# Third chunk's scores by seven half products, projected rows in two copies a buffer, two or three softening steps a block

## The chip, the cores and the metric

The kernel runs on one core of one Trainium2 chip. The metric is the device time of one execution in microseconds; the median of several runs is compared. Engines are called as in the profile: PE (matmul), PEld (its weight loads), DVE (vector), ACT (scalar), POOL (GpSimd), SP or SyncE (which issues most DMAs). Everything is float32 unless said otherwise.

## The reference

A graph network of four layers over N = 2708 nodes with D = 512 features; `adj` is a sparse 0/1 matrix (about 16 neighbours a node). `_layernorm` is over the features.

```python
deg = max((adj != 0).sum(-1), 1)
x = _layernorm(x + relu((dinv * (adj + I) * dinv @ x + x) @ W0 + b0))  # layer 0, dinv = rsqrt(deg)
x = _layernorm(x + (dis * adj * dis @ x) @ W1.T + b1)                  # layer 1
y = x                                                                  # layer 2: two attention layers
for l in range(2):
    Wh, Ws = split(y @ W_stack[l], 2)
    a = softmax(Wh @ Ws.T) * adj                 # softmax over all 2708, then masked
    y = leaky_relu(a @ Wh + y, 0.01)
x = _layernorm(x + y)
x = _layernorm(x + adj @ (x @ W3) + b3)                                # layer 3, heads side by side
```

## The kernel before, in words

**Tiles.** The 2708 nodes are 22 blocks of 128 rows (the last has 20). They are also cut into six chunks of columns, `CH`: four of 512, one of 384, one of 276; indices k = 0 to 5, so the "third chunk" is k = 2. SBUF is handed out in 87 pages of 128 x 512 floats (`page`), eleven wider ones (`wide`) for gathered rows; PSUM is two groups of four banks (`bank`). `Ordered` keeps the order in which instructions are issued on each engine, so every engine runs them in the order of the Python program.

**Layers 0, 1 and 3** are products with the adjacency, chunk by chunk (`step`, `multiply`), in two float32r halves (xh and xl times m, the mask turned to float32r by ACT). `finish` and `normalizing` do the layer norm of a chunk's blocks.

**An attention layer** (`Attention.layer`) goes over the chunks of destination nodes. For a chunk, `walk` yields the score matrix, transposed, source block by source block: 22 pages `s`, 128 sources x up to 512 destinations each. A block "directly" is four matmuls (`scores`; each shows as two records in the profile), copied from PSUM by ACT. In chunks of the list `SEVEN` (before: k = 0 and 1) two blocks at a time are made by seven half products in place of eight (`pair_steps`, Strassen's scheme: `PRODUCTS`, sums s1 to s4 of the projected weights and t1 to t4 of the moving side, made or loaded once). There PE's results x (product by product) and y pass through ACT copies, and DVE adds them: `first_block` adds y from PSUM to s, `second_block` adds v to r. Block 18 and the last, of 20 rows, are done directly also there.

**What goes on beside the scores.** `walk` yields "end" after each block and, in seven-product chunks, also "mid" between products. At "end" number n, `layer` lets the chunk before (`old`) go on: maxima of its blocks (`greatest`), at n = 2 PE's transposes `tr_top` and DVE's reduction `mx` and copy `wide` (`shift_rows`), at n = 4 the transposes `tr_mx` of `wide` into a tile `shift` (`shift_columns`); then the chunk joins `to_soften`. A step of `soften` is, on DVE, a subtraction of `shift` from block v, ACT's exponential of block v - 3, DVE's sum and multiplication with the mask of block v - 4, and the store of that block (`pairs<-s`, queue of SP). A chunk needs 26 steps. How many are issued is written out by hand:

```python
if what == "mid":
    self.soften_next(); self.weigh(); continue
...
many = 2 if len(self.to_soften) > 1 else 1 + n % 2
for _ in range(0 if ch.seven else many):
    self.soften_next()
```

**Gathers.** Row j of the DRAM buffer `pairs` holds, for source j, its projected row z (512 floats) and its masked scores towards the chunk's four blocks of destinations, z standing three times between the scores so that z and any 128 scores are one piece of memory. There are two buffers a layer, used by chunks in turn; `store_z` writes z into both. When a chunk is softened wholly, `fetch` gathers with POOL's indirect DMA, 128 listed sources at a time (12 gathers for a block of destinations), up to ten ahead; `weigh` multiplies a gathered tile's scores with its z on PE into `acc`. It only does so when a clock kept by the program (`advance`) says that the tile should have landed. `end` finishes a block of destinations on DVE: times the softmax's divisor, plus the residual `xr`, leaky ReLU; in the second layer also plus the old row block x1 (`first`), loaded by `weigh` with a block's first product, and statistics.

**Ends of the layers.** In the last chunk and behind it, a generator `fill` gives PE other work: the second attention layer's projections (`second`, `project_steps`, which read the first layer's output, transposed by `turn` 8 us of program clock after a chunk's end), or layer 3's first steps (`early`). Loads for `early` go out at n = 5, 11 and 19 of the last chunk.

**Names in the profile.** All work is recorded under line 71 (a helper), so tiles are told apart by name: `sp`, `spx`, `spy` are scores, `acc<-g` gathered products, `acc<-m,xh` and `xl` layers 0, 1, 3; `wst` and `z` projections.

Of the kernel before, what the change touches and what calls it, by code (L numbers as in the profile page):

```python
# [505 lines left out]
ALONE = 18  # L506
SEVEN = [0, 1]
PROJECTED = [0, 1]
# [44 lines left out]
class Fast:  # L553
# [18 lines left out]
    def run(self):  # L572
        kernel, nc = self.k, self.nc
        with ExitStack() as ctx:
# [37 lines left out]
            for some in (parts[:-1], parts[-1:]):  # L612
                made = []
                for i, n, ps in some:
                    made.append((i, n, self.combine(ly, k, len(made), i, n, ps)))
                for _ in self.finish(ly, k, made):
                    pass
# [27 lines left out]
    def early(self, run):  # L645

        seq = run.seq
        yield True
        self.load(*seq[0])
        self.load(*seq[1])  # L650
        yield True
        self.prepare(*seq[0])
# [47 lines left out]

    def normalizing(self, mv, rows):


        nc, small = self.nc, self.small
        m = len(rows)
        y = small.tile([P, DC], FP, tag="y", name="y")[:, :m]
        yield from self.rsqrt(y, mv[:, :m, 1], LN_EPS)
        for q, (r, o, n) in enumerate(rows):
            nc.vector.tensor_scalar(
                o[:n], r[:n], mv[:n, q, 0:1], y[:n, q : q + 1], ALU.subtract, ALU.mult  # L710
            )
# [532 lines left out]

    def finish(self, ly, k, parts):
# [7 lines left out]
        work = self.normalizing(ly.mv[k], [(x, o, n) for (_, n, x), (_, o, _) in zip(parts, out)])  # L1253
# [62 lines left out]
    def step(self, run, t):  # L1316

        ly, k, g = run.seq[t]
        self.other = (k + 1) % 2
        if run.before and run.phase == 2:  # L1320
            next(run.finish)
        self.before_products(run, t)
        if ly.number == 0 and (k, g) == (1, 0):
# [101 lines left out]
    def index(self, k):  # L1425
# [74 lines left out]
        yield "PE"  # L1500
        rank = ranks("rest", rest, up)
        yield "DVE"
# [81 lines left out]
class Chunk:  # L1584


    def __init__(self, ly, k):
# [4 lines left out]
        self.half = self.cw // 2  # L1592
        self.seven = k in SEVEN
        self.part, self.complete, self.ready, self.top = {}, [], [], None
# [24 lines left out]
class Attention:  # L1619
# [7 lines left out]
    def __init__(self, fast):  # L1627
# [10 lines left out]
            [  # L1638
                self.scratch.tile([NP, 2 * PAIR + D], FP, tag=f"p{a}{b}", name=f"pairs{a}{b}")
                for b in range(2)  # L1640
# [22 lines left out]
        self.left = None  # L1663
        self.to_soften = []


    def blank(self):

        t, n = self.page("blank"), NP - N
        self.nc.gpsimd.memset(t, 0.0)  # L1670
        for pairs in (p for ly in self.pairs for p in ly):
            self.nc.sync.dma_start(
                pairs[N:, : 2 * PAIR + D].rearrange("j (r d) -> j r d", d=D),
                t[:n, :].unsqueeze(1).to_broadcast([n, (2 * PAIR + D) // D, D]),
            )
# [176 lines left out]
    def store_z(self, ly, i, n, z):  # L1852
        for b in range(2):
            rows = ly.pairs[b][i * P : i * P + n, :]
            self.nc.sync.dma_start(
                bass.AP(rows.tensor, rows.offset, [rows.ap[0], (PAIR, 3), (1, D)]),
                z[:n].unsqueeze(1).to_broadcast([n, 3, D]),
            )
# [40 lines left out]
    def in_turn(self, pairs, a, b, ly=None, k=None):  # L1899
# [7 lines left out]
        for n, what in enumerate(order):  # L1907
# [4 lines left out]
            else:  # L1912
# [3 lines left out]
                if not t["left"]:  # L1916
                    t["left"] = "-"
                    self.total(t)
                    for i, z in zip(t["blocks"], t["to"]) if ly else ():
                        self.store_z(ly, i, P, z)  # L1920
            if n == len(order) - 4 and ly:
                self.sum_xt(ly, k + 1)
# [160 lines left out]
    def pair_steps(self, ch):  # L2083
# [6 lines left out]
        groups = [p[0] for p in pairs if p[0] < STREAMED and p[1] == 0]  # L2090
        following = ch.k + 1 in SEVEN

# [18 lines left out]
        def six(t):  # L2111
            self.product(ch, t, 3, t["y"][:, h:cw])
            self.product(ch, t, 6, t["x"])
            nc.scalar.copy(t["s"][:, h:cw], t["x"])

        def seven(t):
# [9 lines left out]
        def first_block(t):  # L2126
            nc.vector.tensor_add(t["s"][:, :cw], t["s"][:, :cw], t["y"][:, :cw])
            ch.complete.append(t["j"][0])
# [5 lines left out]
        for n, p in enumerate(pairs):  # L2134
# [9 lines left out]
            if older:  # L2144
                four(older)
            if ch.k and p[1] == 0 and p[0] + 1 in groups:
                self.load_sums(ch.ly, p[0] + 1)
            if following and p == pairs[-2]:
                self.load_sums(ch.ly, 0)
# [134 lines left out]
    def soften(self, ch):  # L2284
# [30 lines left out]
        to = ch.ly.pairs[ch.k % 2][j * P : j * P + n, :]  # L2315
        if cw == BANK:
            nc.sync.dma_start(
                to[:, : 2 * PAIR].rearrange("j (r x) -> j r x", x=PAIR)[:, :, D:],
                ch.s[j][:n, :].rearrange("j (r x) -> j r x", x=2 * P),
            )  # L2320
            return
        for r in range(2):
            w = min(2 * P, cw - r * 2 * P)
            nc.sync.dma_start(
                to[:, r * PAIR + D : r * PAIR + D + w],
                ch.s[j][:n, r * 2 * P : r * 2 * P + w],
            )

# [16 lines left out]
    def fetch(self, ch):  # L2345
# [6 lines left out]
        for b in (q, q + 1):  # L2352
            self.load_rows(ch, b)

        h = t // ONLY if t < QUARTERS * ONLY else (QUARTERS - 1, 0)[q % 2]
        first, width = (D + P + h * QW, D + P - h * QW) if q % 2 else (0, D + (h + 1) * QW)
        self.nc.gpsimd.indirect_dma_start(
# [39 lines left out]
    def weigh(self, wait=False):  # L2397
# [16 lines left out]
        if first:  # L2414
            ch.acc = self.bank(1, f"acc{ch.name}_{q}")
            if ch.ly.number == 1:
                ch.first[q] = self.page(f"x1{ch.name}_{q}")
                self.nc.sync.dma_start(ch.first[q][:w], self.k.saved[1][ch.blocks[q][0]][:w])
        for h, g in enumerate(gs):
            lo, m = (0, w) if len(gs) == 1 else (h * QW, QW)  # L2420
            e, z = (0, P - lo) if q % 2 else (D + lo, 0)
            nc.tensor.matmul(
# [13 lines left out]
    def end(self, ch, q, acc, x, first):  # L2436
# [19 lines left out]
        if q == len(ch.blocks) - 1:  # L2456
            self.later(
                8,
                lambda: self.f.turn(
                    ch.ends, ch.k, 1, f"x2b{ch.k}", self.k.turned[1][ch.k], nc.sync  # L2460
                ),
            )

# [60 lines left out]
    def layer(self, ly, chunks, fill):  # L2524
        f = self.f
        self.chunks, self.made = chunks, {}
        for k, ch in enumerate(chunks):
# [4 lines left out]
            for what in self.walk(ch):  # L2532
# [9 lines left out]
                if old and n < 2:  # L2542
                    self.greatest(old, last=n == 1)
                many = 2 if len(self.to_soften) > 1 else 1 + n % 2
                for _ in range(0 if ch.seven else many):
                    self.soften_next()
# [61 lines left out]
    def second(self, first):  # L2608
# [87 lines left out]
```

## Time and profile before

| | |
|---|---|
| median of 3 runs | 2239.82 us (2239.29 to 2243.12) |
| profiled execution, its own time | 2235.33 us |
| its span, first to last instruction | 2233.6 us |
| PE busy | 2196.9 us (98%), granted clock 0.995 on average |
| DVE / ACT / POOL busy | 1590.0 (71%) / 771.7 (35%) / 711.8 us (32%) |
| DMA | 502.29 MB, 225 GB/s on average |
| first attention layer's scores | from 738.6 us |
| second attention layer's scores | from 1406.6 us |

In the page's slices each digit is one fortieth of the span (55.8 us) and gives busy tenths. A line of a timeline is: start, length, engine, line, operation, tiles, shape, count, and in brackets the idle time ahead of it with what ended it. A line of the waits is: waiting engine and tile, what it waited for, total us, times, longest.

### The profile page before, as it was taken

Reading aid. Unit: us, or ns where it says so; the run is one execution under the profiler, and the core shown is the slowest. Engines: PE = TensorE matmul, PEld = TensorE weight load, DVE = VectorE, ACT = ScalarE, POOL = GpSimd, SP = SyncE. Lnnn points to the kernel's source line nnn. Section 1 sums busy time; section 2 is a strip of 40 time slices with the busy share of each in tenths; the row PEclk is TensorE's granted clock in tenths of the full one; section 3 lists DMA queues with packets and bytes.
Section 4 is the critical chain, followed back from the end, with each engine's and each line's share of the span. In section 5 each row is a group of like instructions: output and inputs, shape, how many; then the busy total and the mean of one; then the engine's idle time right before and its main releaser. Section 6 shows DMA issues by size and latency. Waiting matters only on the chain.

```text
span 2233.6 us, 29413 instructions
## 1 busy us (share of the span) xinstructions
PE 2196.9 (98%) x9652; PEld 1504.0 (67%) x9652; DVE 1590.0 (71%) x3342; ACT 771.7 (35%) x1687; POOL 711.8 (32%) x827
## 2 busy tenths in 40 slices
PE   9999999999999999999999999999999997999997
PEld 6677788889877887443555776886443564477896
DVE  6777888887887869856777832469868887445734
ACT  7444363333333234222322422234322333342121
POOL 2333541111000000556466551000666565643000
PEclk9999999999999999999999999999999998999999
DMA  9986761222467615889699999714879799884321
GB/s 340 282 228 171 190 191 65 88 79 93 151 260 290 231 34 157 273 293 327 227 358 360 349 391 367 259 48 144 300 273 331 261 320 344 305 258 132 105 76 43
DMA packets 273619, 502.29 MB, mean 225 GB/s; under 512 B 41646, under 2 KB 133478, under 8 KB 273456
## 3 DMA queue, kind: packets, MB, share of 16 engines
q1 hardware_dynamic: 204800, 285.36, 36.8%
q0 software_dynamic: 68656, 214.96, 29.1%
q8 instruction: 78, 1.28, 0.2%
q14 instruction: 85, 0.70, 0.1%
HBM read 314.37 MB, written 185.83 MB: 224 GB/s over the span
## 4 chain that ended last, share of the span: by engine, by line
PE 87%; DMA 7%; DVE 3%; ACT 1%; SPq 1%; issue 1%; POOL 0%; DVEq 0%; ACTq 0%; POOLq 0%
PE acc L71 33%; PE sp L71 22%; PE spx L71 6%; PE spy L71 5%; PE mm L71 3%; PE mmx L71 3%; PE mmy L71 2%; DMA at<-in_adj_t 2%; PE z_0x L71 2%; PE wst L71 1%; PE wst_0x L71 1%; PE z_0y L71 1%; PE wst_1x L71 1%; PE z_1x L71 1%; DMA xt<-t 1%; DMA x<-in_x 1%
## 5 line engine op out<-in xcount | busy, mean ns | idle before, releaser
L71 POOL DMA_INDIRECT g<-pairs,givers x510 | 530.4, 1040 | 805.6 <-DMA pairs<-s 240.9
L71 PE MATMUL acc<-m,xh 128*128 128x512 f32 (+4 forms) x1584 | 564.3, 377 | 9.9 <-ACT m L71 8.9
L71 PE MATMUL acc<-m,xl 128*128 128x512 f32 (+4 forms) x1584 | 549.3, 365 | 4.1 <-DVE xl L71 4.1
L71 PE MATMUL sp<-xs,wst_sb 128*128 128x512 f32 (+4 forms) x1440 | 511.4, 521 | 0.0
L71 PEld LDWEIGHTS sp<-xs,wst_sb 128*128 128x128 f32 (+1 forms) x1440 | 256.1, 185 | 243.5 <-issue 164.5
L71 PEld LDWEIGHTS acc<-m,xh 128*128 128x128 f32 (+1 forms) x1584 | 287.9, 188 | 71.1 <-issue 17.0
L71 PEld LDWEIGHTS acc<-m,xl 128*128 128x128 f32 (+1 forms) x1584 | 288.2, 188 | 46.7 <-DVE xl L71 4.8
L71 PE MATMUL acc<-g 128*32 128x512 f32 (+1 forms) x1020 | 269.2, 606 | 4.3 <-DMA g<-pairs,givers 3.8
L71 ACT COPY s<-sp 128x512 f32<-128x512 f32 (+2 forms) x172 | 88.0, 511 | 460.4 <-PE sp L71 443.7
L71 ACT CAST m<-at 128x512 fp32r<-128x512 uint8 (+5 forms) x396 | 200.5, 566 | 60.6 <-DMA at<-mask 28.3
L71 DVE TENSOR_TENSOR sum<-sum,s 128x512 f32<-128x512 f32 (+4 forms) x252 | 156.8, 622 | 64.6 <-ACT s L71 64.4
L71 PEld LDWEIGHTS acc<-g 128*32 128x32 f32 (+1 forms) x1020 | 76.4, 135 | 147.2 <-issue 105.9
L71 DVE TENSOR_TENSOR s<-s,a 128x512 f32<-128x512 f32 (+3 forms) x264 | 165.8, 628 | 9.1
L71 DVE TENSOR_TENSOR s<-s,shift 128x512 f32<-128x512 f32 (+3 forms) x264 | 161.5, 619 | 2.1 <-ACT shift L71 2.1
L71 DVE TENSOR_TENSOR top<-top,s 128x512 f32<-128x512 f32 (+3 forms) x240 | 149.0, 621 | 8.9 <-ACT s L71 7.0
L71 ACT ACTIVATE s<-s 128x512 f32<-128x512 f32 (+3 forms) x264 | 144.5, 578 | 26.4 <-DVE s L71 26.2
L71 POOL DMA_DIRECT2D x<-o x44 | 25.4, 585 | 298.2 <-DVE o L71 254.2
L71 PE MATMUL mm<-w,ht 128*128 128x512 f32 (+1 forms) x240 | 98.8, 594 | 0.0
L71 ACT ACTIVATE rs_t<-rs_v 128x4 f32<-128x4 f32 (+3 forms) x31 | 6.4, 205 | 256.8 <-DVE rs_v L71 256.8
L71 DVE SCALAR_TENSOR_TENSOR odd<-at 128x512 bf16<-128x512 f32 (+2 forms) x132 | 82.2, 623 | 8.2 <-DMA at<-in_adj_t 6.2
L71 POOL DMA_DIRECT2D mask<-some x72 | 43.4, 610 | 136.9 <-ACT some L71 128.4
L71 DVE SCALAR_TENSOR_TENSOR xr<-acc,rden,xr 128x512 f32<-128x512 f32 (+1 forms) x44 | 32.8, 746 | 63.4 <-PE acc L71 63.1
(345 smaller groups left out, 2926.7 us busy)
## 6 DMA issues: line engine op xcount, KB each, us to landing
pairs<-z_sb SPq DMA_DIRECT2D x84, 768.0 KB
pairs<-s SPq DMA_DIRECT2D x168, 256.0 KB
at<-in_adj_t SPq DMA_DIRECT2D x84, 256.0 KB
xres<-x POOLq DMA_DIRECT2D x44, 256.0 KB, 4.4
x<-o POOLq DMA_DIRECT2D x43, 256.0 KB, 3.2
pairs<-s SPq DMA_DIRECT2D x84, 128.0 KB
a<-mask SPq DMA_DIRECT2D x40, 256.0 KB
x<-x SPq DMA_DIRECT2D x37, 256.0 KB
```

What stands on the lines that cost most here:

```text
L71: ins = call(*args, **kw)
```

## The change

- `SEVEN` is now a list for each layer and holds k = 0, 1 and 2 for both; `sums` s1, s2, s4 are loaded for k = 1 and 2. In a seven-product chunk with k > 1, softening steps are issued also at "end".
- Steps at an "end" of a direct chunk: two if the first chunk waiting is `old`, else three; one or two less in a seven-product chunk.
- In `pair_steps`, ACT copies y to a page u, and `first_block` adds u in place of y.
- A row of `pairs` holds z twice: s0 z s1 s2 z s3. A block of a full chunk is stored in pieces of 128 floats in place of 256; `store_z` writes two copies; the gather's offsets follow.
- x1 is loaded in `fetch`, ahead of a block's first gather, and no longer in `weigh`.
- `turn` is marked when issued; `second` makes it be issued (`need_turned`) before the loads that read it, and loads further ahead when it is. In layer 2's second half `sum_xt` comes two products later.
- In `index`, ACT copies the second rank to a page. In `step`, tiles are prepared ahead of the normalization's next part. `early`'s second load comes with the third call. At the very end, the norm of all but the last block is applied by ACT.

```diff
-SEVEN = [0, 1]
+SEVEN = ([0,1,2],[0,1,2])
...
-                for _ in self.finish(ly, k, made):
+                for _ in self.finish(ly, k, made, scalar=len(some) > 1):
...
         self.load(*seq[0])
+        yield True
         self.load(*seq[1])
-        yield True
         self.prepare(*seq[0])
...
+        if scalar:
+            b = small.tile([P, DC], FP, tag="mx", name="less")[:, :m]
+            nc.vector.scalar_tensor_tensor(b, mv[:, :m, 0], -1.0, y, ALU.mult, ALU.mult)
+            for q, (r, o, n) in enumerate(rows):
+                nc.scalar.activation(
+                    o[:n], r[:n], AF.Identity, bias=b[:n, q : q + 1], scale=y[:n, q : q + 1]
+                )
+            return
...
+        self.before_products(run, t)
         if run.before and run.phase == 2:
             next(run.finish)
-        self.before_products(run, t)
...
-        rank = ranks("rest", rest, up)
+        rank = self.page(f"rank_r{k}", FP, one)
+        nc.scalar.copy(rank, ranks("rest", rest, up))
...
-        self.seven = k in SEVEN
+        self.seven = k in SEVEN[ly.number]
...
-                self.scratch.tile([NP, 2 * PAIR + D], FP, tag=f"p{a}{b}", name=f"pairs{a}{b}")
+                self.scratch.tile([NP, 2 * PAIR], FP, tag=f"p{a}{b}", name=f"pairs{a}{b}")
...
-                bass.AP(rows.tensor, rows.offset, [rows.ap[0], (PAIR, 3), (1, D)]),
-                z[:n].unsqueeze(1).to_broadcast([n, 3, D]),
+                bass.AP(rows.tensor, rows.offset + P, [rows.ap[0], (PAIR, 2), (1, D)]),
+                z[:n].unsqueeze(1).to_broadcast([n, 2, D]),
...
-            if n == len(order) - 4 and ly:
+            if ly and n == len(order) - (2 if ly.number else 4):
                 self.sum_xt(ly, k + 1)
...
+            t["u"] = self.page(f"u{t['name']}")
+            nc.scalar.copy(t["u"][:, :cw], t["y"][:, :cw])
...
-            nc.vector.tensor_add(t["s"][:, :cw], t["s"][:, :cw], t["y"][:, :cw])
+            nc.vector.tensor_add(t["s"][:, :cw], t["s"][:, :cw], t["u"][:, :cw])
...
-            if ch.k and p[1] == 0 and p[0] + 1 in groups:
+            if ch.k in (1, 2) and p[1] == 0 and p[0] + 1 in groups:
                 self.load_sums(ch.ly, p[0] + 1)
-            if following and p == pairs[-2]:
+            if following and ch.k < 2 and p == pairs[-2]:
                 self.load_sums(ch.ly, 0)
...
         if cw == BANK:
+            four = [to.ap[0], (PAIR, 2), (P + D, 2), (1, P)]
             nc.sync.dma_start(
-                to[:, : 2 * PAIR].rearrange("j (r x) -> j r x", x=PAIR)[:, :, D:],
-                ch.s[j][:n, :].rearrange("j (r x) -> j r x", x=2 * P),
+                bass.AP(to.tensor, to.offset, four),
+                ch.s[j][:n, :].rearrange("j (r b x) -> j r b x", r=2, b=2),
             )
             return
...
+        if ch.ly.number == 1 and q not in ch.first:
+            ch.first[q] = self.page(f"x1{ch.name}_{q}")
+            self.nc.sync.dma_start(ch.first[q][:w], self.k.saved[1][i][:w])
+
+        h = t // ONLY if t < QUARTERS * ONLY else (0, QUARTERS - 1)[q % 2]
+        first, width = (P, D + (h + 1) * QW) if q % 2 else (h * QW, D + P - h * QW)
...
-            if ch.ly.number == 1:
-                ch.first[q] = self.page(f"x1{ch.name}_{q}")
-                self.nc.sync.dma_start(ch.first[q][:w], self.k.saved[1][ch.blocks[q][0]][:w])
...
-                many = 2 if len(self.to_soften) > 1 else 1 + n % 2
-                for _ in range(0 if ch.seven else many):
+                many = 2 if self.to_soften[:1] == [old] else 3
+                if ch.seven:
+                    many = (many - 1 if n % 2 else many - 2) if k > 1 else 0
+                for _ in range(many):
                     self.soften_next()
...
+            self.need_turned(k + 1)
             self.load_xt(ly, k + 1)
-            if 0 < k < STREAMED - 2:
+            if k > 0 and k + 2 in self.turned:
                 self.load_xt(ly, k + 2)
```

More of the change, by code (lines that the diff above doesn't have):

```diff
@@ L699, in normalize, with normalizing @@
             pass
-    def normalizing(self, mv, rows):
+    def normalizing(self, mv, rows, scalar=False):
         nc, small = self.nc, self.small
@@ L1243, in sum, with finish @@
         return x
-    def finish(self, ly, k, parts):
+    def finish(self, ly, k, parts, scalar=False):
         nc, out = self.nc, []
@@ L1252, in finish @@
             out.append((i, o, n))
-        work = self.normalizing(ly.mv[k], [(x, o, n) for (_, n, x), (_, o, _) in zip(parts, out)])
+        rows = [(x, o, n) for (_, n, x), (_, o, _) in zip(parts, out)]
+        work = self.normalizing(ly.mv[k], rows, scalar)
         next(work)
@@ L1663, in __init__ @@
         self.left = None
-        self.to_soften = []
+        self.to_soften, self.turned = [], set()
     def blank(self):
@@ L1672, in blank @@
             self.nc.sync.dma_start(
-                pairs[N:, : 2 * PAIR + D].rearrange("j (r d) -> j r d", d=D),
-                t[:n, :].unsqueeze(1).to_broadcast([n, (2 * PAIR + D) // D, D]),
+                pairs[N:, : 2 * PAIR].rearrange("j (r d) -> j r d", d=D),
+                t[:n, :].unsqueeze(1).to_broadcast([n, 2 * PAIR // D, D]),
             )
@@ L2090, in pair_steps @@
         groups = [p[0] for p in pairs if p[0] < STREAMED and p[1] == 0]
-        following = ch.k + 1 in SEVEN
+        following = ch.k + 1 in SEVEN[ch.ly.number]
         def begin(n, p):
@@ L2316, in soften @@
         if cw == BANK:
+            four = [to.ap[0], (PAIR, 2), (P + D, 2), (1, P)]
             nc.sync.dma_start(
-                to[:, : 2 * PAIR].rearrange("j (r x) -> j r x", x=PAIR)[:, :, D:],
-                ch.s[j][:n, :].rearrange("j (r x) -> j r x", x=2 * P),
+                bass.AP(to.tensor, to.offset, four),
+                ch.s[j][:n, :].rearrange("j (r b x) -> j r b x", r=2, b=2),
             )
             return
[L2322 to L2327, printed above, removed]
+        nc.sync.dma_start(to[:, :P], ch.s[j][:n, :P])
+        nc.sync.dma_start(to[:, P + D : D + cw], ch.s[j][:n, P:cw])
     def divisor(self, ch):
@@ L2353, in fetch @@
             self.load_rows(ch, b)
-        h = t // ONLY if t < QUARTERS * ONLY else (QUARTERS - 1, 0)[q % 2]
-        first, width = (D + P + h * QW, D + P - h * QW) if q % 2 else (0, D + (h + 1) * QW)
+        if ch.ly.number == 1 and q not in ch.first:
[3 more added lines that the diff above has]
+        first, width = (P, D + (h + 1) * QW) if q % 2 else (h * QW, D + P - h * QW)
         self.nc.gpsimd.indirect_dma_start(
@@ L2415, in weigh @@
             ch.acc = self.bank(1, f"acc{ch.name}_{q}")
-            if ch.ly.number == 1:
-                ch.first[q] = self.page(f"x1{ch.name}_{q}")
-                self.nc.sync.dma_start(ch.first[q][:w], self.k.saved[1][ch.blocks[q][0]][:w])
         for h, g in enumerate(gs):
             lo, m = (0, w) if len(gs) == 1 else (h * QW, QW)
-            e, z = (0, P - lo) if q % 2 else (D + lo, 0)
+            e, z = (D + lo, 0) if q % 2 else (0, P - lo)
             nc.tensor.matmul(
@@ L2456, in end, with turn, need_turned @@
         if q == len(ch.blocks) - 1:
[L2457 to L2462, printed above, removed]
+            self.later(8, lambda: self.turn(ch))
+    def turn(self, ch):
+        self.f.turn(
+            ch.ends, ch.k, 1, f"x2b{ch.k}", self.k.turned[1][ch.k], self.nc.sync
+        )
+        self.turned.add(ch.k)
+    def need_turned(self, k):
+        while k < len(CH) and k not in self.turned:
+            if self.pending:
+                self.pending.pop(0)[1]()
+            else:
+                assert self.weigh(True)
     def normalize(self, ch):
```

## The prediction

> **What bounds the kernel now.** I read the page first: its busy rows, its slices and the waits of PE.
>
> ```profile
> span 2233.6 us, 29413 instructions
> PE 2196.9 (98%) x9652; PEld 1504.0 (67%) x9652; DVE 1590.0 (71%) x3342; ACT 771.7 (35%) x1687; POOL 711.8 (32%) x827
> PE   9999999999999999999999999999999997999997
> PEclk9999999999999999999999999999999998999999
> DMA  9986761222467615889699999714879799884321
> ...
> PE acc L71 <- ACT m L71: 8.9, 3, 7.8
> PE acc L71 <- DVE xl L71: 4.1, 1, 4.1
> PE acc L71 <- DMA g<-pairs,givers: 3.8, 9, 0.9
> ```
>
> PE works 2196.9 of 2233.6 us, so the path to the end is PE's instruction stream plus 36.7 us of gaps. About 13 of these are the tail behind the last matmul. The only large gap before that is in slice 34, and there the granted clock dips too. The table by stage places it, and shows two stages that the change touches:
>
> ```profile
> 805.00:871.00 66.00, 66.00 (x306) 55.62 (x305) 52.61 (x89) 27.71 (x66) 0.00 (x0) 1.00 0.33 104
> 888.00:905.00 17.00, 17.00 (x41) 7.49 (x40) 16.76 (x28) 5.02 (x10) 3.27 (x2) 1.00 0.44 145
> 1856.00:1890.00 34.00, 21.82 (x76) 12.57 (x75) 23.22 (x46) 13.38 (x28) 18.55 (x18) 0.80 0.99 356
> ```
>
> Columns: length, busy PE, PEld, DVE, ACT, POOL, clock, DMA share, GB/s. 805 to 871 is the second chunk of the first attention layer, already by seven products: PE without a gap. 888 to 905 lies in its third chunk: PE full, but DVE busy 16.76 of 17. 1856 to 1890 is the end of the second layer: PE idle 12.2 us, clock 0.80. The chain of waits and the timelines of DVE and PE say why:
>
> ```profile
> 1856.69 15.02 DMA x<-x
> ```
>
> ```profile
> 1860.85 0.69 DVE L71 SCALAR_TENSOR_TENSOR r<-xr 128x512 f32<-128x512 f32 x1
> 1871.80 0.69 DVE L71 TENSOR_TENSOR r<-r,x 128x512 f32<-128x512 f32 x1 [10.26 <-DMA x<-x]
> ```
>
> ```profile
> 1877.05 0.79 PE L71 MATMUL acc<-m,xh 128*128 128x512 f32 x1 [7.81 <-ACT m L71]
> 1881.94 0.80 PE L71 MATMUL acc<-m,xl 128*128 128x512 f32 x1 [4.11 <-DVE xl L71]
> ```
>
> `weigh` issues the load of the old row block x1 only with the block's first gather product; it took 15.02 us on a full DMA (share 0.99). `end` adds it on DVE, which stood 10.26 us; ACT stood behind DVE, and PE behind both.
>
> **The change, part by part** (against the profiled execution, 2235.33 us, span 2233.6).
>
> *Products.* A direct block is 8 matmul records in 3.43 us, so two take 6.87. One product of the seven starts 0.864 us after the one before, so a pair of blocks takes 6.04. Saved: 0.82 x 10 pairs x 2 layers = **-16.4**. The second chunk shows that PE can run such a chunk without gaps.
>
> *DVE at the start of the third chunk.* This is where I expect part of it back.
>
> ```profile
> 859.01 0.68 DVE L71 TENSOR_TENSOR s<-s,shift 128x512 f32<-128x512 f32 x1
> 859.61 0.68 DVE L71 TENSOR_TENSOR sum<-sum,s 128x512 f32<-128x512 f32 x1
> 860.33 0.69 DVE L71 TENSOR_TENSOR s<-s,a 128x512 f32<-128x512 f32 x1
> 860.94 0.68 DVE L71 TENSOR_TENSOR s<-s,shift 128x512 f32<-128x512 f32 x1
> ...
> 884.81 0.43 DVE L71 COPY wide<-mx 128x512 f32<-128x512 f32 x1
> ```
>
> One softening step is 1.93 us of DVE (859.01 to 860.94). Ten steps of the first chunk are left over when the third begins at 871.10 (26, less one at each of the 16 "mid" yields after its softening starts; the groups of 805 to 871 have 16 subtractions of `shift`). Before, 4 of them are issued ahead of the copy `wide`, which ended at 885.2, and the transposes `tr_mx` that need it began at 887.31, 2.1 us later. After, `many` and the "mid" yields issue 1+1+2+1+1 = 6 ahead of it, the 20-row total of the last block moves ahead of it (2.7 us), and two subtractions for t3 join (0.7). Less the 2.0 us that DVE idled there before: 885.2 + 3.86 + 2.7 + 0.7 - 2.0 = 890.5. PE gets there after 11 products (9.5), the lone block (3.43), the 20-row block (0.97), the transposes of top (0.43) and the four left over (0.86): 871.1 + 15.2 = 886.3. So PE waits 4.2 us with every later product queued behind, in each layer: **+8.4** (bounds: 0, if DVE is earlier by what it idles later in the stage; 6 each, without the idle time taken off).
> Behind that wait the clock matters. The row of 1.73 us (`tr_top` behind `top`, at 1891.45) left matmuls at 0.23 us, the 7.81 and 4.11 left them at 0.43 until 1887.9. 4.2 lies between; I take no loss, and 3 each as the far end.
> The Trainium skill (TensorE: Matmul & The Clock Gate, Part 1) speaks against the change here: an idle window of about 3.4 us halves the clock until a busy window has passed. By it an estimated 1.7 us would be added to each wait, 3.4 in all.
>
> *DVE for the rest of it.* Per pair DVE has three steps (5.79), two sums (0.60 and 0.33) and two maxima (1.33), 8.05 us, against 6.04 of PE until the gathers' products join, about 38 us in; with them PE needs 9.1 (16.1 us for three direct blocks and one gathered block before, so 5.4/16.1 of PE is gathers) and DVE 8.9. The first steps of a chunk only subtract, so DVE's lag starts at 7.8 us and grows to 8 to 9. ACT's exponential follows three steps behind, 6.04 us, and PE bears 2.2 more: a stall of some 1 us. SyncE's queue adds to it: the loads of s1, s2, s4 (12 more a layer, 0.45 us each) stand behind stores that wait for this DVE, are needed two pairs (12 us) later, and pages are scarcer by t1 to t4, the sums, `u` and `v`. I take 2.5 a layer: **+5** (bounds 0 and 20: ten a layer, if page, store and load all follow DVE's lag). The copy to `u` (ACT 0.59, in place of the 0.68 add from PSUM) goes free: ACT is under half busy, and it frees the bank without DVE. If ACT had no room it would cost 10 x 0.59 a layer.
>
> *x1 moved to `fetch`.* It is now issued ten or eleven gathers ahead (1.26 us each on POOL's timeline, so 13 us), beside the residual `xr`, whose loads stop nobody in this stage. It costs SyncE no further issue, the gathers on POOL's queue do not wait for it, and it holds a page 13 us longer. The two waits (11.9), the 1.73 behind, and the half clock (about 3) are 16.7 us at stake, and 3.8 on gathers. What is late next: POOL, at 1.26 us a gather from 1895 without a gap, and the fifth chunk's softening; two or three steps a block from the third chunk on bring both forward, by four blocks each. I take **-13** (bounds 0 and -21).
>
> *Two or three steps a block in chunks 4 to 6.* Direct blocks: 2 x 1.93 + 0.60 + ends against PE 5.17 balances; for the 384-wide fifth DVE needs about 4.8 against 3.9, for the last 3.8 against 2.8. Over 13 blocks the lag is 12 us; three further score banks and the 1.5 blocks to the exponential cover 12 to 17. **+2** (0 to 8).
>
> *DMA.* From the trace's packet records: a 1,024-byte packet of the hardware queue takes 46 ns (median), 512 bytes 27 ns, 2,048 bytes 84 ns. Score rows of the four full chunks become 86,656 packets of 512 in place of 43,328 of 1,024: (86,656 x 27 - 43,328 x 46) / 16 = +21.7 us of all 16 engines. Two copies of z for three: 10,832 x 84 / 16 = -56.9. Sums loaded again: 24 x 128 x 84 / 16 = +16.1. Net -19, in stages where PE waits for a transfer 1.5 us in all: **0** (-1.5 to +3).
> The skill (DMA: Bandwidth & Descriptors, "Why small descriptors are slow") charges 3 cycles a packet on 32-byte beats: 38 cycles for 35, 9% more on these stores where the rows make it 17%; by it the store term would be an estimated 11 us.
>
> *The rest.* The rank copied to a page, prepared tiles ahead of the square root: the waits of 1.0 on `place_r` and 1.1 on `m` go, **-1** (-2 to +1). The last normalization on ACT: 0.99 of DVE leaves the tail and 0.17 comes, **-0.8**. The later `turn` and `need_turned`, and `early`'s shifted yields only reorder: 0 (-1 to +2; their cover is layer projection work on a full PE).
>
> Sum: -16.4 + 8.4 + 5 - 13 + 2 + 0 - 1 - 0.8 = **-15.8**, or 2219.5 against 2235.3. The median shown is 2239.82, 4.5 above the profiled run, so I forecast 2239.8 - 15.8 = **2224**.
>
> **Rivals.**
> *DVE hides everything (faster still).* No wait at `tr_mx` and no lag: -16.4 - 13 + 0 - 1.8 = -31, 2209. For it: DVE's 2 us of idle at that place. Against: its 16.76 of 17.
> *DVE sets the third chunk's pace (slower).* Its work there is 58 (90 softening operations at 0.645) + 12.7 (21 maxima) + 9.3 (the pairs' sums) + 4.5 (20-row total, reduction of top, t3) + 3.8 (block ends) = 88 us, plus the 10.8 that `sum` waited for ACT in the groups of 871 to 962: 99. PE has 67.5 of products and others and a third of its time for gathers from 38 us on: (67.5 - 0.336 x 38) / 0.664 = 82. If PE follows, each layer loses 17: 34 - 16.4 - 1.8, and with half the gain at the end, -6.5: +9, 2249. For it: the full DVE and the scarce pages; against: with a DVE that lags, ACT is early and the 10.8 vanish. It decides from 15.6 us lost a layer (9.1 with no gain at the end).
> *The wait at the end only moves.* PE then meets the gathers at POOL's 1.26 us for 0.86 of work: -16.4 + 13.4 + 2 - 1.8 = -3, 2237. For it: DMA 0.93 and POOL without a gap after 1895; against: POOL had stood 10.57 us in the very stall.
>
> **How the numbers follow.** Forecast 0.45 (2214 to 2233), all hidden 0.22 (2203 to 2214), DVE's pace 0.18 (2241 to 2262), moved wait 0.15 (2232 to 2243). Faster by over 0.2% (4.5 us, about what can be told from no change): 0.45 + 0.22 + 0.05 of the moved wait = 0.72; same 0.09; slower 0.19. The range 2206 to 2244 leaves out some 0.07 of the second case and most of the third. By itself the forecast spans 2214 to 2233.
>
> **What would show it.** Right: PE busy near 2180; records of sp<-xs,wst_sb and its kin down by 320, seven's up; "DVE r <- DMA x<-x" gone and PE's wait for m under 2 us; two new PE waits of 2 to 6 us at `tr_mx` behind `wide`; z stores of 512 KB. Wrong: PE waits for ACT or a sums load through the third chunk (DVE's pace), or a slice 34 as idle as now behind another releaser (moved wait).

## The result, and the profile after

| | before | after |
|---|---|---|
| median of 6 runs each | 2239.56 us (2237.22 to 2243.12) | 2232.64 us (2230.54 to 2234.45) |
| ratio | | 0.9972, 95% interval 0.9962 to 0.9982 |
| profiled execution (span) | 2235.33 (2233.6) | 2232.52 (2230.8) |

The change makes the kernel faster by 6.9 us as the medians have it and by 6.3 (0.28%) as the ratio has it; 15.8 were forecast. The experiments ran in five groups, each with its own runs of the kernel before, and times are compared within a group only: before took 2238.72 us in the second group, as here, and 2266 to 2272 in the other four, with more waits round the projections.

The page and PE's waits after, as shown of before (`...` stands for lines left out, here and in the code):

```profile
span 2230.8 us, 30237 instructions
PE 2187.0 (98%) x9892; PEld 1554.8 (70%) x9892; DVE 1614.4 (72%) x3397; ACT 817.7 (37%) x1815; POOL 721.0 (32%) x827
PE   9999999999999998999999999999999999899997
DMA  9976762222446415989799896515899899973221
...
PE tr_mx L71 <- DVE wide L71: 15.1, 3, 5.3
PE acc L71 <- DMA g<-pairs,givers: 8.1, 12, 1.8
PE wst_0y L71 <- DVE s1mixed L71: 2.6, 1, 2.6
```

PE is busy 9.9 us less, but the span is only 2.8 shorter: gaps came. The waits for `m` (8.9) and `xl` (4.1) are gone; three waits at `tr_mx` (15.1), more for gathered tiles (8.1, was 3.8) and one at the start of the second layer's projections are new. Slice 16 of PE's row has lost its nine: that is the first layer's third chunk. The same three stages as before, shifted by what the kernel is early or late there (columns as in the prediction):

```profile
801.00:867.00 66.00, 66.00 (x306) 55.63 (x305) 52.33 (x91) 32.42 (x76) 0.00 (x0) 1.00 0.31 96
884.00:901.00 17.00, 12.22 (x50) 10.62 (x51) 16.66 (x29) 6.47 (x16) 2.48 (x3) 0.80 0.53 162
1862.00:1896.00 34.00, 31.29 (x120) 18.25 (x119) 29.63 (x59) 11.29 (x25) 25.37 (x24) 0.90 1.01 353
```

The second chunk is as it was. In the third, PE stands 4.8 of 17 us and the clock falls to 0.80 while DVE stays full. At the end of the second layer PE now stands 2.7 us in place of 12.2. DVE's and PE's timelines in the third chunk:

```profile
888.29 0.43 DVE L71 COPY wide<-mx 128x512 f32<-128x512 f32 x1
```

```profile
888.78 1.12 PE L71 MATMUL tr_mx<-ident,wide 128*128 128x128 f32 x4 [5.25 <-DVE wide L71]
889.69 1.91 PE L71 MATMUL spy<-xs,wst_sb 128*128 128x256 f32 x4
891.39 1.75 PE L71 MATMUL spy<-t,s 128*128 128x256 f32 x4
892.98 1.03 PE L71 MATMUL spx<-xs,wst_sb 128*128 128x256 f32 x4
```

PE waits 5.25 us (4.2 forecast), and then two products start 1.70 and 1.59 us after the one before instead of 0.864, the transposes before them take 0.91 for 0.43: 2.05 us lost to the half clock, where I had taken none.

### The profile page after: what moved, and what is told of

Same layout as the page of the kernel before. It is cut to its first block, busy times and chain, and to the rows that moved or that the text cites. A ratio compares the mean times of both kernels' runs of the same rounds, so it can differ in the third digit from the quotient of the medians.

```text
span 2230.8 us, 30237 instructions
## 1 busy us (share of the span) xinstructions
PE 2187.0 (98%) x9892; PEld 1554.8 (70%) x9892; DVE 1614.4 (72%) x3397; ACT 817.7 (37%) x1815; POOL 721.0 (32%) x827
## 4 chain that ended last, share of the span: by engine, by line
PE 89%; DVE 6%; DMA 4%; issue 1%; ACT 0%; POOL 0%; SPq 0%; DVEq 0%; POOLq 0%; ACTq 0%
PE acc L71 37%; PE sp L71 14%; PE spx L71 8%; PE spy L71 6%; PE mm L71 4%; PE mmx L71 3%; DVE s L71 2%; DMA g<-pairs,givers 2%; PE mmy L71 2%; PE z_0x L71 2%; PE wst L71 2%; PE z_0y L71 1%; PE z_1x L71 1%; PE wst_0x L71 1%; PE mix L71 1%
## 5 line engine op out<-in xcount | busy, mean ns | idle before, releaser
L71 POOL DMA_INDIRECT g<-pairs,givers x510 | 539.4, 1058 | 795.6 <-issue 308.8
L71 PE MATMUL sp<-xs,wst_sb 128*128 128x512 f32 (+4 forms) x1120 | 374.0, 503 | 0.0
L71 PEld LDWEIGHTS sp<-xs,wst_sb 128*128 128x128 f32 (+1 forms) x1120 | 196.5, 184 | 172.8 <-issue 93.0
L71 ACT COPY s<-sp 128x512 f32<-128x512 f32 (+2 forms) x132 | 64.3, 488 | 349.4 <-PE sp L71 343.4
L71 ACT COPY s<-spx 128x256 f32<-128x256 f32 x180 | 66.9, 372 | 121.0 <-PE spx L71 119.9
L71 PE MATMUL spx<-xs,wst_sb 128*128 128x256 f32 x320 | 82.4, 381 | 1.1 <-DVE xs L71 1.1
```

Of the source, the lines that this page charges most:

```text
L71: ins = call(*args, **kw)
```

## Experiments

### First group: single edits, each way

Before took 2266.13 us here (35 runs).

```diff
 # e1_two_chunks: the kernel after with
-SEVEN = ([0,1,2],[0,1,2])
+SEVEN = ([0,1],[0,1])
 # e2_early: the kernel after with, in early,
+        self.load(*seq[1])
         yield True
-        self.load(*seq[1])
 # e3_wide_first: the kernel after with, in layer,
+                    if k > 1 and n <= 2:
+                        many = 0
+                    elif k > 1 and n <= 6:
+                        many += 1
 # e4_x1_only: the kernel before, x1 loaded in fetch, not in weigh
```

> The kernel after, with the third chunk's scores direct again in both layers; all else stays. Theory A (the products' gain of 16.4 us was eaten in the third chunk itself by two waits of 5.25 us at tr_mx and about 2 us of half clock behind each): within 2 us of the kernel after, about 2232 to 2235. Theory B (forecast: waits and lag cost 13.4 of the 16.4, the rest went elsewhere): 3 us slower than after, 2236. Rival C (the third chunk keeps its whole gain and the loss lies in other edits): 14 to 16 us slower than after, 2247 to 2249. If the seven products cost more than they save (a lag beyond the waits), it is faster than after by 3 to 8.

> The kernel after, with the second load of the last layer's rows issued again with the second call, as before. Theory A (this one moved load makes the new wait of 4.63 us at tr_mx near 1908 us, and the half clock behind it): that wait gone, 6 to 9 us faster than after, about 2225. Rival B (the DMA queues are full there, and another transfer is late in its place, for example a gathered tile or x1): 0 to 2 us faster, with a new wait of PE of some 4 us between 1890 and 1925.

> The kernel after, with no softening step at the ends 0 to 2 of the third chunk and one more at each of the ends 3 to 6, so that four steps fewer (7.7 us of DVE) stand ahead of the copy wide. Theory A (the wait at tr_mx and the clock lost behind it are the price of the steps ahead of it): both waits of 5.25 us gone, 10 to 15 us faster than after, about 2219. Rival B (DVE's queue as a whole sets the stage; the work only moves behind): the waits gone from tr_mx but others of 2 to 6 us later in the chunk (ACT or sums), 0 to 4 us faster or slower.

> The kernel before, with only the load of x1 moved to the fetch of a block's first tile. Theory A (forecast's term): the waits of 7.81 and 4.11 us at the end of the second layer gone, 13 us faster than before, about 2227 (0 to 21). Rival B (the wait moves to gathered tiles or to POOL): the end of the layer as long as before, 0 to 3 us faster.

Measured, as ratios to before: e1 0.9996 (0.9976 to 1.0016), e2 1.0018 (0.9998 to 1.0039), e3 1.0051 (1.0027 to 1.0076), e4 0.9960 (0.9940 to 0.9981). The kernel after was not in this group, so e1 and e2 say little by themselves, but e1's trace says something I had not thought of. With direct scores, PE waits at `tr_mx` in the third chunk all the same (PE's timeline):

```profile
890.18 0.68 PE L71 MATMUL tr_mx<-ident,wide 128*128 128x128 f32 x4 [4.49 <-DVE wide L71]
```

The new rule alone, three steps at each block end while an older chunk waits, puts nine steps ahead of `wide`. So the rule is an edit with a price of its own in the third chunk; neither e5 below, with the old steps, nor the kernel before has a wait there. In e3 the steps behind `wide` come back: the wait in the first third chunk is gone, but there and in the second layer the list of PE's waits has

```profile
PE spy L71 <- ACT s L71: 10.9, 4, 2.8
PE spx L71 <- ACT s L71: 4.0, 1, 4.0
PE spy L71 <- DMA s<-sums: 3.1, 2, 2.4
```

and it is slower than e2, the kernel after but for early's load (which costs nothing that can be measured, as the fourth group shows): rival B. e4 is 9 us faster than before (4 to 14), between its two theories.

### Second group: the edits at the softened chunks

```diff
 # c_after: the kernel after itself
 # e5_no_third: the kernel after with SEVEN = ([0,1],[0,1]) and
-                many = 2 if self.to_soften[:1] == [old] else 3
...
+                many = 2 if len(self.to_soften) > 1 else 1 + n % 2
+                for _ in range(0 if ch.seven else many):
 # e6_third_only: the kernel before with the third chunk in SEVEN, u, and the new rule
 # e7_old_direct_steps: the kernel after with, for chunks that are not by seven products,
+                else:
+                    many = 2 if len(self.to_soften) > 1 else 1 + n % 2
```

> The kernel after itself, beside the other three on one chip, as their measure. Expected: a ratio of 0.997 to the kernel before (0.9962 to 0.9982 as first measured).

> The kernel after without its two edits at the softened chunks: the third chunk's scores direct, and the steps a block as before; the load of x1, the layout, the ranks and all else of the change stay. Theory A (third chunk and step rule together cost what they save, or more): 0 to 8 us faster than after. Forecast's terms (-16.4 + 8.4 + 5 + 2 = -1): 1 us slower than after. Rival (the products keep most of their gain, and the loss lies elsewhere): 10 to 16 us slower.

> The kernel before with only these two edits: the third chunk by seven products (with ACT's copy of y) and the new number of steps a block. Theory A: 2 to 8 us slower than before, with both waits of about 5 us at tr_mx in the third chunk, and the end of the second layer still waiting for x1. Forecast's terms: 1 us faster than before. Rival (keeps its gain): 10 to 16 us faster.

> The kernel after with the steps at the blocks of direct chunks as before (two if more than one chunk waits, else one and two in turn), the third chunk's as after. Theory A (three steps a block put a lag on DVE ahead of wide and behind the gathers in chunks four to six, about 4 us a layer): 4 to 8 us faster than after. Forecast's term (+2): 2 us faster. Rival (fewer steps bring the gathers later and the end of each layer with them): 2 to 8 us slower.

| | median, us | ratio to before (2238.72) |
|---|---|---|
| c_after | 2233.29 | 0.9977 (0.9968 to 0.9985) |
| e5_no_third | 2229.24 | 0.9957 (0.9945 to 0.9969) |
| e6_third_only | 2242.56 | 1.0014 (1.0005 to 1.0024) |
| e7_old_direct_steps | 2235.27 | 0.9986 (0.9976 to 0.9995) |

Without the two edits that give the change its name the kernel is 4.0 us faster than after; by themselves they make the kernel before 3.8 us slower (1 to 5). Theory A holds. e7 parts them: third chunk with old steps 6.0 us slower than e5, new rule on top of it 2.0 us faster, not slower as I expected; the two intervals overlap, so this 2.0 is hardly clear of zero, unlike its two parts below. The profiled executions show where, counted between PE's transposes `tr_top` (first of the first layer, first of the second, end):

| us | before | c_after | e7 | e5 |
|---|---|---|---|---|
| up to the first layer's first `tr_top` | 815.0 | 811.8 | 811.1 | 812.3 |
| from there to the second layer's first | 665.6 | 676.5 | 669.9 | 666.5 |
| PE idle in it | 1.6 | 13.3 | 8.8 | 2.4 |
| from there to the end | 753.0 | 743.8 | 750.5 | 747.8 |

*Third chunk (e7 against e5):* +3.4 in the first layer, +2.7 in the second. In the first: PE idle +6.4; half clock about +2.05, as above; gathered products, the same 510 records, +2.9 as PE's groups have it (e5, then e7):

```profile
L71 PE MATMUL acc<-g 128*32 128x512 f32 (+2 forms) x510 | 129.6, 604 | 2.4 <-DMA g<-pairs,givers 2.1 <-DVE top L71 0.2
```

```profile
L71 PE MATMUL acc<-g 128*32 128x512 f32 (+2 forms) x510 | 132.5, 605 | 2.9 <-DMA g<-pairs,givers 2.7
```

PE's busy time is 3.0 less in all (661.1 for 664.1), so the products themselves saved 3.0 + 2.05 + 2.9 = 7.9, near the 8.2 forecast. Of the 2.9, some 1.2 lie in the third chunk; 1.9 lie behind the last `tr_top`, where the first layer's projections are, in the same 112 records (e5, then e7), and why is not shown:

```profile
L71 PE MATMUL acc<-g 128*32 128x512 f32 x112 | 16.4, 605 | 1.0 <-DMA g<-pairs,givers 1.0
```

```profile
L71 PE MATMUL acc<-g 128*32 128x512 f32 x112 | 18.3, 605 | 0.2
```

*New rule (c_after against e7):* +6.6 in the first layer, -6.7 in the second. Gathers come earlier in both. In the first they had a long stage of projections to hide in (some 166 records behind the last `tr_top` in e7, 142 in c_after). With fewer left there PE reaches a product that needs DVE's `s1mixed` 17.0 us behind that `tr_top`, for 21.4 in e7, and DVE, with softening steps of the last chunk ahead, starts on `s1mixed` after 19.3 us, for 15.3. PE waits 2.8 us and loses the clock again, about 1.6 us by the two starts behind it (DVE's and PE's timelines of c_after, then of e7):

```profile
1242.25 0.75 DVE L71 TENSOR_TENSOR s1mixed<-mixed,mixed 128x256 f32<-128x256 f32 x2
```

```profile
1242.72 2.08 PE L71 MATMUL wst_0y<-t1x,s1mixed 128*128 128x256 f32 x4 [2.76 <-DVE s1mixed L71]
1244.59 1.78 PE L71 MATMUL wst_0x<-t2x,s2mixed 128*128 128x256 f32 x4
```

```profile
1228.40 0.41 DVE L71 TENSOR_TENSOR s1mixed<-mixed,mixed 128x256 f32<-128x256 f32 x1
```

```profile
1234.49 1.13 PE L71 MATMUL wst_0y<-t1x,s1mixed 128*128 128x256 f32 x4
```

That is 4.4 of the 6.6; PE also idles 1.8 us more in the third and the sixth chunk, mostly for gathered tiles.

In the second, gathered products that are left stand alone: behind the last `tr_mx` PE has nothing beside them until layer 3's products, 31.8 us in e7 (1896.05 to 1927.88) and 17.9 in c_after (1910.24 to 1928.15), which outweighs c_after's longer wait at that `tr_mx` (8.90 us for 3.64). After the last `tr_top` c_after has 142 records of gathered products, e7 166 (PE's groups of that stretch):

```profile
L71 PE MATMUL acc<-g 128*32 128x512 f32 (+2 forms) x142 | 40.2, 650 | 0.8 <-DMA g<-pairs,givers 0.7
```

```profile
L71 PE MATMUL acc<-g 128*32 128x512 f32 (+2 forms) x166 | 53.2, 648 | 3.0 <-DMA g<-pairs,givers 2.6
```

### Third group: x1, early, the rule by layer, later transposes

```diff
 # e8_x1_only: as e4
 # e9_early_back: e5 with early's two loads together again
 # e10_layer2_steps: e5 with
+                if ly.number == 1 and k > 2:
+                    many = 2 if self.to_soften[:1] == [old] else 3
 # e11_late_columns: the kernel after with
-                if old and n == 4:
+                if old and n == (6 if ch.seven and k > 1 else 4):
                     self.shift_columns(old)
```

> The kernel before with only the load of x1 moved to the fetch, a second time, since the first run of it left an interval of 8 us. Theory A (forecast): 13 us faster than before. Theory B (the gathers' own stream sets the end of the second layer, so that most of the removed waits of 11.9 us come back as waits for gathered tiles or at wide): 3 to 7 us faster than before, with the stretch from the sixth chunk's tr_top to the end 3 to 6 us longer than in the kernel before (342 us).

> The kernel after without the third chunk's products and with the old steps (2229.2 us when run), and with the last layer's second load issued again with the second call. Theory A (the moved load costs a wait of PE at wide of 4 us and half clock behind it): that wait under 1 us, 4 to 7 us faster than without this edit, 2223 to 2225. Theory B (gathers set the end): the wait at wide gone, but the waits for gathered tiles grow by as much, within 2 us of 2229.

> The kernel after without the third chunk's products and with the old steps in the first attention layer, but the new steps (two or three) in chunks four to six of the second layer. Theory A (the new steps lose some 6 us in the first layer, where the gathers have a long stage of projections to hide in, and gain some 6 in the second, whose end waits for gathers): 3 to 6 us faster than with the old steps in both, 2223 to 2226. Rival (the difference between the layers is chance): within 2 us of 2229.

> The kernel after with only the transposes tr_mx of the third chunk issued two block ends later (6 us of PE's products put ahead of them), DVE's steps as they are. Theory A (the wait at tr_mx and the half clock behind it are the loss, 5.25 and about 2 us a layer): both waits gone, 8 to 14 us faster than after, about 2221. Rival B (DVE's queue as a whole is late, so the wait comes back at the next instruction that needs DVE or ACT behind it, as in the run with the steps moved): waits of 2 to 5 us elsewhere in the third chunk, 0 to 4 us faster or slower.

Ratios to before (2271.54): e8 0.9972 (0.9952 to 0.9991), e9 0.9943 (0.9920 to 0.9966), e10 0.9887 (0.9872 to 0.9902), e11 1.0041 (1.0026 to 1.0056).

e8: 6 us. In its trace, as in e4's, one of the two waits that I had put down to x1 is still there: 4.4 us at `acc<-m,xl`, which the traces put down to no releaser ("issue"), with DVE's `xl` queued behind the fifth chunk's last softening steps and no wait of DVE for a transfer; and the stretch from the last `tr_top` to the end is 345.6 us in e4, 346.0 in e8 and 346.0 in e5 of the second group, for 342.2 before. The numbers are theory B's; its cause is so only in part, since the wait that is left is DVE's. e9 can't choose between its theories, as e5 is not in its group. e10: the rule in the second layer alone is worth more than the 3 to 6 us expected, some 8 us by medians and 13 by ratios against e9, which differs from it also in early's loads.

e11: the wait at `tr_mx` in both third chunks is gone and the kernel no faster (after itself had 1.0029 in the next group). PE waits a few products on, for sums that SyncE could load only after stores that wait for DVE (SP's timeline, then PE's):

```profile
886.10 9.81 SPq L71 DMA_DIRECT2D pairs<-s  x6
...
896.96 1.37 SPq L71 DMA_DIRECT2D s<-sums  x3
```

```profile
901.77 1.20 PE L71 MATMUL spy<-t,s 128*128 128x256 f32 x4 [3.08 <-DMA s<-sums]
```

### Fourth group: less work for DVE, and a better version

```diff
 # c_after_again: the kernel after itself
 # e14_no_masks: the kernel after, while the third chunk is walked without (scores go on unmasked)
-        nc.vector.tensor_mul(s, s, ch.masks.pop(j)[:n, :cw])
 # e13_layer2_steps: as e10
 # e12_both: e13 with early's two loads together again
```

> The kernel after itself, as the measure of the other three on the same chip. Expected: 0.997 to 0.998 of the kernel before.

> The kernel after with the multiplications by the mask left out of the softening steps that run beside the third chunk (the scores go to the gathers unmasked), so that DVE has 0.68 us a step less, some 4 us ahead of wide and 16 in the chunk; the order of all else stays. Theory A (DVE's load is what eats the products' gain): the waits at tr_mx fall from 5.25 to 1 to 2 us, the half clock behind them goes, and the kernel is 8 to 12 us faster than after. Rival B (ACT, the banks, or the loads of the sums set the stage): the waits go but others of 2 to 5 us take their place, 0 to 3 us faster.

> The kernel after without the third chunk's products, with the old steps in the first attention layer and the new ones in chunks four to six of the second. Theory A (the new steps gain some 6 us at the second layer's end and lose as much in the first layer): 8 to 11 us faster than after, 0.993 of before. Rival: 4 us faster than after, as with the old steps in both.

> The kernel of the run with the new steps in the second layer alone, with the last layer's second load issued with the second call again. Theory A (the moved load costs 4 us of waiting at wide and the half clock behind it): 4 to 7 us faster than that run. Theory B (the gathers set the end of the layer): the wait at wide under 1 us, the waits for gathered tiles longer, and the time within 2 us of that run.

| | median, us | ratio to before (2272.42) |
|---|---|---|
| c_after_again | 2279.51 | 1.0029 (1.0008 to 1.0050) |
| e14_no_masks | 2271.15 | 0.9995 (0.9976 to 1.0013) |
| e13_layer2_steps | 2252.08 | 0.9898 (0.9875 to 0.9922) |
| e12_both | 2251.12 | 0.9904 (0.9879 to 0.9930) |

e14 is some 8 us faster than after, as theory A had it: with 0.68 us of DVE less a step, the waits at `tr_mx` are 1.90 and 1.62 us. From `tr_top` to `tr_top` (c_after_again, then e14; first layer):

```profile
877.56:983.56 106.00, 95.61 (x398) 63.81 (x397) 87.78 (x145) 36.97 (x87) 56.30 (x54) 0.97 0.91 308
```

```profile
877.01:978.93 101.92, 97.35 (x397) 63.91 (x396) 68.21 (x114) 37.10 (x87) 61.27 (x55) 0.98 0.96 318
```

PE works about as long (97.35 us for 95.61), stands 4.6 us for 10.4, and DVE's busy time falls by 19.6. With e3 and e11, where only the order was changed and nothing was gained, this says that DVE's load, not its order, is what eats the products' gain; rival B is refuted for this stage.

e12 equals e13 (0.9904 and 0.9898): early's moved load costs nothing that can be measured. Its wait at `tr_mx` is in the traces (4.63 us after, 8.90 in c_after, 3.85 in e13, none in e12), but gathered tiles land meanwhile; in e12 PE waits for these instead (7.7 us in all in the list of waits, `acc` for `g`; 3.0 in e13).

In this group the change as it stands is 0.29% slower than before. So its sign depends on the group. e13 is 20 us faster than before and 27 faster than after, where 8 to 11 were expected; e10, which is the same kernel, was as far below before in the third group.

### Fifth group

e15_x1_only is e4, e16_both is e12.

> The kernel before with only the load of x1 moved. Theory (one of the two waits, 7.8 us, was x1's; the one of 4.1 at xl is DVE's own backlog of the fifth chunk and stays; the gathers' stage behind it grows by some 3.6): 5 to 9 us faster than before, with a wait of 2 to 4.5 us at acc<-m,xl near 1880 us. Forecast: 13 us faster.

> The kernel after without the third chunk's products, the old steps in the first layer, the new ones in the second, and the last layer's second load as before. Expected: 0.990 to 0.994 of the kernel before, 2217 to 2225 us where the kernel before takes 2239.

Before took 2268.89. e15 0.9981 (0.9961 to 1.0001), 4 to 6 us where 5 to 9 were expected, again with the wait that x1 doesn't explain:

```profile
1912.09 0.79 PE L71 MATMUL acc<-m,xl 128*128 128x512 f32 x1 [4.47 <-DVE xl L71]
```

e16 0.9939 (0.9918 to 0.9960). So the best version (third chunk direct, old steps in the first layer, new ones in the second, all else of the change; early's load either way) is at 0.989 to 0.994 of before in four runs. It was not run in the second group; there e5, with the old steps in both layers, took 2229.24.

## Why the prediction was right or wrong

The direction was right, and the time lies in the range, but with luck: two misses the other way (items 3 and 5) hid part of the losses, and the gain was less than half of the forecast. The sum step by step, measured in the second group (medians, where nothing else is said):

| step | forecast | measured |
|---|---|---|
| products | -16.4 | -15.8 (2 x 7.9, from PE's busy time in the first layer) |
| wait at `tr_mx` and DVE's lag | +8.4 and +5 | +21.9 (e7 less e5 is +6.0 to +6.1) |
| new number of steps | +2 | -2.0 (+6.6 and -6.7 by layer) |
| x1, ranks, tail and all else | -14.8 | -9.5 (e5 against before) |
| sum | -15.8 | -5.4 (c_after against before) |

1. *Products: right.* 320 records of direct scores went, and the saving is the forecast one.
2. *DVE at the start of the third chunk: right place, mis-sized by 8.5 us.* Six steps ahead of `wide` and the wait behind them came as counted, 5.25 for 4.2. What failed is the sentence "I take no loss, and 3 each as the far end": it is 2.05 a layer. There the rule that I had cited from the Trainium skill (TensorE: Matmul & The Clock Gate, Part 1) was nearer: the estimated 1.7 from it is close to the measured loss, and my interpolation between rows was not. The other part is the 2.5 a layer for the rest of the chunk: further waits of some 1.2 us, and 2.9 us more on gathered products, 1.2 of them in this chunk, which I had not priced at all.
3. *Two or three steps a block: "+2 (0 to 8)" hid two effects of 6.6.* I priced DVE's lag in chunks 4 to 6 alone, and not what earlier gathers do to each layer's end. That the end of the second layer gains, I had half said (under x1); that the first layer's projections lose the gathers that filled them, and that DVE comes later to `s1mixed` there, I had not.
4. *x1: the step that failed is "the two waits (11.9), the 1.73 behind, and the half clock".* Only the wait of 7.81 was x1's. The 4.11 at `xl` stood behind DVE's own backlog: before, DVE was idle until 1871.80 and then worked without a gap until `xl` (its timeline before):

```profile
1881.21 2.49 DVE L71 SCALAR_TENSOR_TENSOR xl<-x,xh 128x512 fp32r<-128x512 f32 x4
```

   Three runs with x1 alone give 0.9960, 0.9972 and 0.9981, some 4 to 9 us, not 13; and the stretch behind the last `tr_top` is 3.4 to 3.8 us longer in e4, e8 and e5. Of these only e5 ran in the second group, and it has other edits too, so what fills that stretch is not shown. The rival "the wait at the end only moves" was partly true.
5. *Start: better than said.* The first `tr_top` comes 2 to 4 us earlier with the changed ranks and order (810.9 after for 815.0 before; 811.1 to 812.3 in the second group for 814.2 in e6, which has the old ones), where I had -1. Which of these edits does it was not tried.
6. *Early's loads and the DMA layout at 0.* Early: right (e12, e13), though the trace of after made it look like 4.6 us and a half clock. The layout was not tried by itself.

The rivals: nothing was hidden as in the first. "DVE sets the third chunk's pace" named the cause: its price, 17 a layer, was too high, but 11 a layer is more than the products save. It was to decide from 15.6 a layer with the whole gain at the end and from 9.1 with none; the loss lies between, and so did that gain, so the change stayed just faster here, and in the fourth group it did not.

Still open: why the change gains 0.23% in the second group and loses 0.29% in the fourth. The first group and the second ran on a chip of the same number, so which chip it is does not settle it.

## What to carry to other kernels

A cheaper product on the bound engine pays only if the engine that feeds the next step has room in that very stage: count its queue from the start of the stage, and try it by taking work away, since work moved only moves the wait. Two waits side by side may have two causes: before a removed stall is counted whole, look whether the engine named in the second was idle or busy. An edit of the order of gathers is worth opposite things in two places, so price it by the end of each stage, and apply it where they stand alone at that end.

## What the runs showed of the hardware

- PE can lose its clock behind short waits. After 1.90 us at `tr_mx` in e14 the next product took 1.71 us from start to start for 0.864:

```profile
884.69 0.78 PE L71 MATMUL tr_mx<-ident,wide 128*128 128x128 f32 x4 [1.90 <-DVE wide L71]
885.26 1.91 PE L71 MATMUL spy<-xs,wst_sb 128*128 128x256 f32 x4
886.97 1.49 PE L71 MATMUL spy<-t,s 128*128 128x256 f32 x3
```

  Not every such wait does it. Behind 2.76 us in the first third chunk of e3 the clock stayed at 1.00 (PE's timeline, then the stretches up to the end of the wait and behind it):

```profile
890.49 1.13 PE L71 MATMUL spy<-xs,s 128*128 128x256 f32 x4 [2.76 <-ACT s L71]
```

```profile
887.00:890.50 3.50, 0.74 (x5) 0.32 (x3) 3.43 (x7) 2.05 (x5) 0.00 (x0) 1.00 0.49 149
890.50:894.00 3.50, 3.50 (x16) 3.11 (x17) 3.40 (x6) 1.59 (x5) 0.00 (x0) 1.00 0.51 153
```

  What decides between the two is not shown. The periods at half clock in the traces' clock records, but for the last of each trace, are 3.41, 6.83, 10.24 or 13.65 us long, all multiples of 3.413. The Trainium skill (TensorE: Matmul & The Clock Gate, Part 1) gives a window of that length; that waits half as long can be enough is not to be read from its rule for idle windows.
- The change's ratio was 0.9977 in one group and 1.0029 in another, with the same median times of DMA packets in the two traces of the kernel after (27 ns for 512 bytes, 84 for 2,048). A verdict on 0.3% holds for the group of runs that it was taken in.
